# Strassen's scheme for the values' products of layers 2 and 3, with a limit on the ratio of the softmax sums

## The chip, the cores and the metric

One core of a Trainium2 chip runs the whole program. The metric is the device time of one execution, in microseconds (us).

## The reference

Four layers act on x of 2 images, 512 channels and 32 x 32 pixels, in float32. Layer 0 is a deformable attention block with an MLP, layer 1 an attention of eight heads. The change concerns layers 2 and 3, attentions of one head over 1024 pixels:

```python
# layer 2
xn = _group_norm(x, gamma, beta)
q, k, v = split(einsum('oc,bchw->bohw', w_qkv, xn) + b_qkv)
attn = softmax(einsum('bci,bcj->bij', q, k) * C ** (-0.5), axis=-1)
out = einsum('bcj,bij->bci', v, attn)
x = x + einsum('oc,bchw->bohw', w_proj, out) + b_proj
# layer 3
q = einsum('dc,bcn->bdn', wq, f) + bq      # 64 rows; wq, wk, wv ~ 0.05 * normal
k = einsum('dc,bcn->bdn', wk, f) + bk
v = einsum('dc,bcn->bdn', wv, f) + bv
attn = softmax(einsum('bdi,bdj->bij', q, k), axis=1)      # no scale
x = gamma * einsum('bci,bij->bcj', v, attn) + x
```

## The kernel before

The program has three parts. `layer0` (L137) does layer 0's attention; `layers` (L1043) does its MLP and layers 1 to 3; `general` (L851) is a second way of doing layers 1 to 3, and is entered only if a flag says so. In `layer0` and `layers` each engine issues its instructions in the order in which the code writes them (`in_order`, L59). In `general` the framework chooses each engine's order.

`layers` takes the exponentials of the scores without subtracting a maximum. With one image at a time, layer 2 computes scores for eight slices of 128 keys (L1551, a product over 512 channels), ScalarE takes their exponentials into four tiles `ps` of two slices each (L1552), and VectorE adds the tiles up (`sums_of`, L1532, and `summed`, L1345) into `acc`. `values` (L1318) has made `vT`, eight slices of keys by 512 channels. In layer 3 `exponentials` (L1409) makes the scores in pairs of 64-row products that lie in the two halves of the array, and the values' products are issued in between (L1581 to L1587).

`weigh` (L1510) then multiplies: for each half of 512 pixels and each of four blocks of 128 channels, eight products over the keys' slices add up in PSUM (L1517, issued by `accumulate`, L135). `reciprocals_of_both` (L1373), called behind the first block, adds `acc` over the partitions on TensorE with a matrix of ones (`den2`), and VectorE takes the reciprocals. VectorE multiplies each block by the reciprocal and adds bias and x (L1523, L1524); in layer 3 a DMA from SP stores it (`store`, L1590). The iterator that `weigh` is lets layer 2's first image advance the second image's group norm (`norms[2]`) between blocks.

`note` (L1352) writes the least and the greatest reciprocal of each `r` into the next column of `span`: eight columns from layer 1 (two images, four pairs of heads; `divide`), two from layer 2, two from layer 3. Before the last block of layer 3, L1597 to L1602 make `lim` 1 on each partition where all reciprocals lie between e^-64 and e^40. A product with ones (`pn`, L1605) counts the partitions, L1606 turns that into `flag` = 128 - count, every engine loads it at L1618, and

```python
    bad = nc.values_load(flag[0:1, 0:1], min_val=0, max_val=P)
    with tc.If(bad != 0):
        with ExitStack() as g:
            general(g)
```

`general` loads x, as it was after layer 0, from a copy in HBM (`x_d`, L855) and all weights anew on SP's queue. It computes layers 1 to 3 with `attend` (L943): for each tile of 128 queries

```python
                    nc.vector.tensor_reduce(nm, sc, AX.X, ALU.max)                                   # L958
                    nc.vector.tensor_scalar(nm, nm, -scale, None, ALU.mult)
                    nc.scalar.activation(p, sc, AF.Exp, bias=nm, scale=scale, accum_out=sm)          # L962
                    nc.vector.reciprocal(sm, sm)
                    nc.gpsimd.tensor_scalar(p, p, sm, 1.0, ALU.mult, ALU.mult)                       # L964
```

stand between the scores (L956; two PSUM buffers, `ps_s`) and eight transposes on TensorE (L969), which ScalarE and VectorE copy in halves (L972, L974) into `pT`; four such tiles are then weighed with the values (L980). In layer 1 it does so for each of the eight heads and both halves of the pixels.

Of the kernel before, what the change touches and what calls it, by code (L numbers as in the profile page):

```python
# [11 lines left out]
F32 = mybir.dt.float32  # L12
AF = mybir.ActivationFunctionType
ALU = mybir.AluOpType
AX = mybir.AxisListType
# [3 lines left out]
P = 128  # L19
B, C, H, W = 2, 512, 32, 32  # L20
HW = H * W
CC = C // P
HALF = 512
# [56 lines left out]
def kernel(ctx: ExitStack, tc: tile.TileContext, a: dict, out: bass.AP):  # L80
    nc = tc.nc
# [3 lines left out]
    wa = ctx.enter_context(tc.tile_pool(name="wa", bufs=1))  # L85
# [16 lines left out]
    xs = []  # L102
# [5 lines left out]
    s2 = const.tile([P, CC], F32, name="s2")  # L108
    nc.vector.tensor_scalar(s2, col("bn2_g", 0, CC), BN_S, None, ALU.mult)

    def load_w(pool, tag, parts):

        w = pool.tile([P, 4 * HID], F32, name=tag, tag=tag)
        views, at = [], 0
        for src in parts:
            k, n = src.shape[0] // P, src.shape[1]
            v = w[:, at : at + k * n].rearrange("p (k n) -> p k n", n=n)
            for kk in range(k):
                nc.sync.dma_start(out=v[:, kk, :], in_=src[kk * P : (kk + 1) * P, :])
            views.append(v)  # L120
            at += k * n
        return views


    def drain(steps):
        for _ in steps:
            pass

    def advance(steps, n=1):
        for _ in range(n):  # L130
            next(steps, None)

    def accumulate(pm, pairs):
        for k, (w, m) in enumerate(pairs):
            nc.tensor.matmul(pm, w, m, start=(k == 0), stop=(k == len(pairs) - 1))  # L135
# [907 lines left out]
    def layers(f, fold_d, t2_b, o2_b):  # L1043
# [3 lines left out]
        small = f.enter_context(tc.tile_pool(name="small", bufs=2))  # L1047
        keep = f.enter_context(tc.tile_pool(name="keep", bufs=1))
        chan = f.enter_context(tc.tile_pool(name="chan", bufs=4))
        ps_m = f.enter_context(tc.tile_pool(name="ps_m", bufs=2, space=PSUM))  # L1050
# [7 lines left out]
        ones = keep.tile([P, P], F32, name="ones1")  # L1058
        nc.gpsimd.memset(ones, 1.0)
        NSUM = 12  # L1060
        span = keep.tile([P, 2, NSUM], F32, name="span")
# [52 lines left out]
        GN_STATS = CC + 3  # L1114
# [6 lines left out]
        with ExitStack() as mlp:  # L1121
# [8 lines left out]
            ps = mlp.enter_context(tc.tile_pool(name="mlp_ps", bufs=3, space=PSUM))  # L1130
# [39 lines left out]
            def product(pm, i, left, right, cols):  # L1170
                l, r = left[i - 1], right[i - 1]
                accumulate(pm, [(l[:, k, cols], r[:, k, :]) for k in range(l.shape[1])])
# [60 lines left out]
            for c in range(MC):  # L1233
                for m in (MC + c, c):
                    pm = ps.tile([P, BLK], F32, name="pmp", tag="pma")
# [4 lines left out]
            for m in (2, 3, 0, 1):  # L1240
                pm = ps.tile([P, BLK], F32, name="pmp2", tag="pmb")
# [4 lines left out]
            for blk in range(1, NBLK):  # L1246
                b = blk * BLK // HW
# [8 lines left out]
                for c in range(MC + 1):  # L1256
                    if c < MC:
                        pms = products(left1, right1, slice(c * P, (c + 1) * P), (1, 2, 6, 7, 5, 4, 3))
                        p1 = first_of(pms)
# [57 lines left out]

        def values(w, h, vT, bias=None, scale=None):  # L1318

            for s in range(8):  # L1320
                pm = ps_m.tile([P, C], F32, name="pmv", tag="mm")
                accumulate(pm, [(h[k][:, s * P : (s + 1) * P], w[:, k, :]) for k in range(CC)])
                if bias is not None:
                    nc.vector.tensor_add(vT[:, s, :], pm, bias)
                elif scale is not None:
                    nc.scalar.mul(vT[:, s, :], pm, scale)
                else:
                    nc.scalar.copy(vT[:, s, :], pm)
                yield
# [22 lines left out]
        def note(r):  # L1352
            i = next(seen)
            nc.vector.tensor_reduce(span[:, 0, i : i + 1], r, AX.X, ALU.min)
            nc.vector.tensor_reduce(span[:, 1, i : i + 1], r, AX.X, ALU.max)

        def divide(o, acc):
# [11 lines left out]
            nc.vector.tensor_mul(o, o, r)  # L1369
            note(r)  # L1370
            yield

        def reciprocals_of_both(acc):  # L1373

            r = rp.tile([P, HW], F32, name="r")
            den = ps_v.tile([P, HW], F32, name="den2", tag="pv")
            for half in range(2):
                n = slice(half * HALF, (half + 1) * HALF)
                accumulate(den[:, n], [(ones, acc[:, part, n]) for part in range(2)])
                nc.scalar.copy(r[:, n], den[:, n])  # L1380
                nc.vector.reciprocal(r[:, n], r[:, n])
            return r

        wb_stack.close()
        fold2 = f.enter_context(tc.tile_pool(name="fold2", bufs=1))
# [5 lines left out]
        outs = f.enter_context(tc.tile_pool(name="outs", bufs=5))  # L1391
# [113 lines left out]
        vT = new_v()  # L1505
        drain(values(v2, h2s[0], vT))
        drain(add_projection(xs[1], proj1, "proj_b", os_[1]))
        q3, k3, v3 = load_w(wa, "wa", [a["wq3"], a["wk3"], a["wv3"]])

        def weigh(x, vT, ps, acc, bias, done):  # L1510

            r = None
            for half in range(2):
                n = slice(half * HALF, (half + 1) * HALF)
                for m in range(CC):
                    pm = ps_m.tile([P, HALF], F32, name="pw2", tag="mm")
                    accumulate(  # L1517
                        pm, [(vT[:, s, m * P : (m + 1) * P], ps[s // 2][:, s % 2, n]) for s in range(8)]
                    )
                    if r is None:  # L1520
                        r = reciprocals_of_both(acc)
                    y = yp.tile([P, HALF], F32, name="y")
                    nc.vector.tensor_mul(y, pm, r[:, n])  # L1523
                    nc.vector.scalar_tensor_tensor(x[:, m, n], y, bias[:, m : m + 1], x[:, m, n], ALU.add, ALU.add)  # L1524
                    done(m, n)
                    if (half, m) == (0, 3):
                        note(r)
                    yield

        yp = f.enter_context(tc.tile_pool(name="yp", bufs=2))  # L1530

        def sums_of(ps):  # L1532
            acc = accp.tile([P, 2, HW], F32, name="acc")
            for j in range(1, len(ps)):
                summed(acc, ps[j], ps[0] if j == 1 else None)
            return acc

        for b in range(B):
            if b == 1:
                drain(t2(1))  # L1540
                vT = new_v()
                drain(values(v2, h2s[1], vT))
            t, h = t2_of[b], h2s[b]
            ps = []
            for s in range(8):
                if s % 2 == 0:
                    ps.append(pp_.tile([P, 2, HW], F32, name="p"))
                sc = ps_s.tile([P, HW], F32, name="score2", tag="s")
                for half in range(2):
                    n = slice(half * HALF, (half + 1) * HALF)  # L1550
                    accumulate(sc[:, n], [(h[k][:, s * P : (s + 1) * P], t[k][:, n]) for k in range(CC)])  # L1551
                nc.scalar.activation(ps[-1][:, s % 2, :], sc, AF.Exp, scale=C ** -0.5)  # L1552
            for _ in weigh(xs[b], vT, ps, sums_of(ps), o2_b, lambda m, n: None):
                if b == 0:
                    next(norms[2], None)


        def project_both(h, r):
# [13 lines left out]
        for b in range(B):  # L1572
            x = xs[b]
            h = [x[:, cc, :] for cc in range(CC)]
            qk = qkp.tile([P, HW], F32, name="qk", tag="qk")
            project_both(h, qk)
            kq = qkp.tile([P, HW], F32, name="kq", tag="qk")
            for lo in (0, 64):
                nc.sync.dma_start(out=kq[lo : lo + 64], in_=qk[64 - lo : 128 - lo])
            vT = new_v()  # L1580
            steps = values(v3, h, vT, scale=col("gamma3"))  # L1581
            advance(steps, 2)
            ps = []
            for j in range(4):
                left = [slice((2 * j + part) * P, (2 * j + part + 1) * P) for part in range(2)]
                ps.append(exponentials((kq, qk), (qk, kq), left, 1.0))
                advance(steps, 1 + j % 2)  # L1587
            acc = sums_of(ps)

            def store(m, n, x=x, b=b):  # L1590
                nc.sync.dma_start(out=out[b, m * P : (m + 1) * P, n], in_=x[:, m, n])

            steps = weigh(x, vT, ps, acc, gb3, store)
            advance(steps, 6)
            if b == 1:

                lim = small.tile([P, 2], F32, name="lim")  # L1597
                nc.vector.tensor_reduce(lim[:, 0:1], span[:, 0, :], AX.X, ALU.min)
                nc.vector.tensor_reduce(lim[:, 1:2], span[:, 1, :], AX.X, ALU.max)
                nc.vector.tensor_scalar(lim[:, 0:1], lim[:, 0:1], float(np.exp(-64.0)), None, ALU.is_ge)  # L1600
                nc.vector.tensor_scalar(lim[:, 1:2], lim[:, 1:2], float(np.exp(40.0)), None, ALU.is_le)
                nc.vector.tensor_mul(lim[:, 0:1], lim[:, 0:1], lim[:, 1:2])  # L1602
                advance(steps)
                pn = ps_v.tile([1, 1], F32, name="pn", tag="pv")
                nc.tensor.matmul(pn, lim[:, 0:1], ones[:, 0:1], start=True, stop=True)  # L1605
                nc.vector.tensor_scalar(flag, pn, -1.0, float(P), ALU.mult, ALU.add)  # L1606
            drain(steps)
# [99 lines left out]
```

## Time and profile before

| | us |
|---|---|
| runs of the kernel | 3490.8, 3491.4, 3492.2 (median 3491.4) |
| the profiled execution | 3489.9 |
| its span, first to last instruction | 3488.1 |
| TensorE busy | 3452.3 |
| VectorE, ScalarE, GpSimd busy | 2477.1, 1756.1, 492.5 |
| layer 2, from the first image's scores | 2990.2 |
| layer 3, from the first image's projection | 3276.0 |

Times in views count from the span's start. A row names line, engine, operation, what it writes and reads by the program's names, shape and count; then its busy time in us and the mean of one in ns; then the engine's idle time ahead of it, and who ended it. A row of the chain of waits has its start, its length and what ran. TensorE's records overlap, so that the pace of a row of products is read from the chain and not from a record's length. A row of a table of windows has the window and its length, the busy us (and instructions) of PE, PE's weight loads, DVE, ACT and POOL, the granted clock, the DMA engines' busy share and GB/s.

### The profile page before, as it was taken

The numbers are of one execution on the slowest core, as the hardware profiler recorded it, in microseconds if no ns is written. First come the engines' busy times: TensorE is split into PE (matmuls) and PEld (weight loads), VectorE is DVE, ScalarE is ACT, GpSimd is POOL, SyncE is SP. The second block draws the span as 40 slices with busy tenths as digits, with TensorE's granted clock in tenths as the row PEclk, the third lists the DMA queues.
The fourth block names the chain that finished last, engine by engine and source line by source line (L and its number), as shares of the span: only waits on it lengthen the run. The fifth ranks groups of instructions, "written<-read, shape, count | busy, mean of one in ns | idle before, by whom it ended". The sixth has DMA issues, their size and how long they took to land.

```text
span 3488.1 us, 58691 instructions
## 1 busy us (share of the span) xinstructions
PE 3452.3 (99%) x24257; PEld 1446.7 (41%) x24257; DVE 2477.1 (71%) x2731; ACT 1756.1 (50%) x2479; POOL 492.5 (14%) x579
## 2 busy tenths in 40 slices
PE   9999999999999999999999999999999999999999
PEld 4333333333333333333333369999433333444443
DVE  7999999999996999999999835455264374130223
ACT  5767867867764868768676612112243242011110
POOL 1222222222221222222222200000001000000000
PEclk9999999999999999999999999999999999999999
DMA  5676676666664666766776620001100000000000
GB/s 173 148 151 141 139 154 137 150 145 138 149 146 94 144 148 133 151 140 141 152 152 139 143 83 9 14 13 56 33 1 0 1 1 0 15 0 0 6 30 25
DMA packets 134067, 313.65 MB, mean 90 GB/s; under 512 B 21152, under 2 KB 66592, under 8 KB 133024
## 3 DMA queue, kind: packets, MB, share of 16 engines
q0 software_dynamic: 56880, 199.79, 30.1%
q1 hardware_dynamic: 76768, 109.50, 9.8%
q8 instruction: 193, 3.16, 0.4%
q14 instruction: 82, 0.67, 0.1%
q10 hardware_dynamic: 144, 0.52, 0.0%
HBM read 65.17 MB, written 10.75 MB: 22 GB/s over the span
## 4 chain that ended last, share of the span: by engine, by line
PE 77%; DVE 16%; issue 4%; ACT 2%; DMA 0%; DVEq 0%; SPq 0%; POOL 0%; ACTq 0%; POOLq 0%
PE z L534 32%; DVE wa L517 6%; PE pw L135 6%; PE pm L1306 5%; PE pma L135 5%; PE pmv L135 5%; DVE h L548 5%; PE pmb L135 4%; PE score L1417 4%; PE score L135 3%; PE pv L1465 3%; DVE h L517 2%; PE ppr L1337 2%; PE pmp L135 2%; PE pp L620 1%
## 5 line engine op out<-in xcount | busy, mean ns | idle before, releaser
L534 PE MATMUL z<-wa,cpb_w 128*32 128x512 f32 x11904 | 1779.1, 593 | 6.7 <-DVE simbias L481 3.4
L543 ACT ACTIVATE h<-z,b2h 128x1024 f32<-128x1024 f32 x1024 | 1135.3, 1115 | 529.6 <-PE z L534 506.1
L534 PE MATMUL z<-h,cpb_w 128*32 128x512 f32 x4480 | 986.3, 593 | 3.4 <-ACT h L543 2.2
L517 DVE CUSTOM_DVE_ANT_1 wa<-tab,tab 128x1024 f32<-128x1024 f32 x744 | 878.5, 1216 | 34.0 <-PE z L534 33.9
L534 PEld LDWEIGHTS z<-wa,cpb_w 128*32 128x32 f32 x11904 | 493.0, 110 | 883.6 <-issue 803.6
L548 DVE SCALAR_TENSOR_TENSOR h<-h,turn,h 128x1024 f32<-128x1024 f32 x512 | 653.6, 1277 | 8.8 <-ACT h L543 8.6
L534 PEld LDWEIGHTS z<-h,cpb_w 128*32 128x32 f32 x4480 | 256.3, 110 | 334.4 <-issue 291.3
L822 POOL DMA_DIRECT2D h<-h x255 | 226.6, 889 | 1060.6 <-DVE h L548 714.8
L517 DVE CUSTOM_DVE_ANT_1 h<-tab,tab 128x1024 f32<-128x1024 f32 x280 | 333.1, 1217 | 11.4 <-PE z L534 11.2
L1418 ACT ACTIVATE p<-score 128x1024 f32<-128x1024 f32 x144 | 139.5, 1021 | 184.8 <-PE score L1417 184.8
L135 PE MATMUL pw<-p,vT 128*128 128x512 f32 x512 | 221.8, 593 | 1.3 <-DVE y L1523 1.3
L1348 DVE TENSOR_TENSOR acc<-acc,p 128x2048 f32<-128x2048 f32 x56 | 128.8, 2300 | 105.1 <-ACT p L1418 57.8
L1201 ACT COPY p<-pma 128x128 f32<-128x128 f32 x70 | 18.6, 265 | 304.1 <-PE pma L135 304.1
L1350 DVE TENSOR_TENSOR acc<-p 128x2048 f32<-128x2048 f32 x12 | 27.5, 2291 | 183.6 <-ACT p L1552 110.0
L815 POOL DMA_DIRECT2D h<-h x126 | 109.0, 865 | 343.4 <-DMA h<-h 339.8
L135 PEld LDWEIGHTS pw<-p,vT 128*128 128x128 f32 x512 | 97.0, 190 | 122.6 <-issue 121.0
L1193 DVE TENSOR_TENSOR upper<-pma,p 128x256 f32<-128x256 f32 x70 | 29.6, 423 | 163.2 <-ACT p L1201 163.2
L819 POOL DMA_DIRECT2D h<-h x126 | 120.2, 954 | 122.5 <-DMA h<-h 117.5
L1108 POOL TENSOR_SCALAR hc<-x,sc,sh 128x1024 f32<-128x1024 f32 x16 | 28.1, 1765 | 706.1 <-DVE sh L1104 509.4
L1417 PE MATMUL score<-q,k 64*128 64x512 f32 x512 | 127.2, 615 | 0.0
L1306 PE MATMUL pm<-hc,wa 128*64 128x512 f32 x512 | 122.4, 603 | 0.0
L1465 PE MATMUL pv<-p,vT 128*64 128x512 f32 x512 | 121.4, 595 | 0.0
(316 smaller groups left out, 3239.3 us busy)
## 6 DMA issues: line engine op xcount, KB each, us to landing
h<-h POOLq DMA_DIRECT2D x255, 512.0 KB, 4.9
h<-h POOLq DMA_DIRECT2D x252, 256.0 KB, 4.9
tab<-slog_d SPq DMA_DIRECT2D x128, 256.0 KB, 4.5
h<-h SPq DMA_DIRECT2D x126, 256.0 KB, 2.3
wa<-in_qkv_w SPq DMA_DIRECT2D x8, 768.0 KB, 7.5
xt<-in_xt SPq DMA_DIRECT2D x8, 512.0 KB, 7.7
wa<-in_mlp_w SPq DMA_DIRECT2D x4, 1024.0 KB, 7.9
wb<-in_mlp_w SPq DMA_DIRECT2D x16, 256.0 KB, 5.5
```

The costliest lines, as they stand in the source:

```text
L135: nc.tensor.matmul(pm, w, m, start=(k == 0), stop=(k == len(pairs) - 1))
L517: nc.vector._custom_dve(TENSOR_ADD_SAT, out=h1.rearrange("p (y x) -> p y x", x=W), in0=tx[:, quad, point, :].unsqueeze(1).to_broadcast([P, ...
L534: nc.tensor.matmul(z[point * 32 : point * 32 + 32, n], cpb_w2[:, lo : lo + 32], h1s[point][:, n], start=True, stop=True,)
L543: nc.scalar.activation(h2, z, AF.Relu, bias=b2h[:, part : part + 1])
L548: nc.vector.scalar_tensor_tensor(h2, h2, turn[:, part // 2 : part // 2 + 1], parts.pop(part + 1), ALU.mult, ALU.add)
L819: nc.gpsimd.dma_start(out=joins[i - 3][1:P:2], in_=joins.pop(i - 2)[1:P:2], accum_op=ALU.add)
L822: nc.gpsimd.dma_start(out=joins[i - 1], in_=other, accum_op=ALU.add)
L1306: nc.tensor.matmul(pm[at : at + wide], w[:, k, lo + at : lo + at + wide], h[k][:, n], start=(k == 0), stop=(k == CC - 1),)
L1348: nc.vector.tensor_add(acc, acc, p)
L1417: nc.tensor.matmul(sc[:, part, :], ks[part][r, left[part]], qs[part][r, n], start=True, stop=True)
L1418: nc.scalar.activation(p[:, :, n], sc, AF.Exp, scale=scale)
L1465: nc.tensor.matmul(pv[part * 64 : part * 64 + 64, n], vT[:, ls, lo : lo + 64], lp[:, part, n], start=(ls == 0), stop=(ls == 7),)
```

## The change

The key slices and the channels on one side, and the pixels on the other, are each split in two: vT into A11 (slices 0 to 3, channels 0 to 255), A12 (slices 4 to 7, channels 0 to 255), A21 and A22 (channels 256 to 511), the exponentials into B11, B12 (slices 0 to 3, pixels 0 to 511 and 512 to 1023), B21 and B22. Seven products of such halves and sums of them replace the eight. VectorE forms the sums of vT (`form_left`), four slices of `spare`, the unused end of the weights' tile, holding three of them and one lying in A21's place; it forms the sums of the exponentials in place, one of them in `spare`; and it adds the products up. `values` makes its slices in the order 0, 4, 1, 5, 2, 6, 3, 7. The second image's group norm advances during the first image's scores. `reciprocals_of_both` goes; its instructions stand in `weigh`, and the second half's reciprocal comes later. A second condition on the reciprocals joins the flag's.

```diff
-            for s in range(8):
+            for s in (0, 4, 1, 5, 2, 6, 3, 7):
...
+        s1v, s2v, s4v = [spare[:, k * HW : (k + 1) * HW].rearrange("p (k n) -> p k n", k=4) for k in range(3)]
+        t2p = spare[:, 3 * HW : 5 * HW].rearrange("p (k n) -> p k n", k=4)
...
+        def form_left(vT, chunks=range(4)):
+            for k in chunks:
+                a11, a21, a12, a22 = vT[:, k, LO], vT[:, k, HI], vT[:, 4 + k, LO], vT[:, 4 + k, HI]
+                nc.vector.tensor_tensor(s1v[:, k], a21, a22, ALU.add)
+                nc.vector.tensor_tensor(s2v[:, k], s1v[:, k], a11, ALU.subtract)
+                nc.vector.tensor_tensor(a21, a11, a21, ALU.subtract)
+                nc.vector.tensor_tensor(s4v[:, k], a12, s2v[:, k], ALU.subtract)
...
+            rights = {
+                1: right(0, n1), 2: right(1, n1), 3: right(1, n2), 4: right(1, n1),
+                5: right(0, n1), 6: [t2p[:, k] for k in range(4)], 7: right(0, n2),
+            }
+            def product(pm, i, m):
+                accumulate(pm, [(lefts[i][k][:, m * P : (m + 1) * P], rights[i][k]) for k in range(4)])
+            def finished(m, n, in0, in1):
+                y = yp.tile([P, HALF], F32, name="y")
+                nc.vector.tensor_tensor(y, in0, in1, ALU.add)
+                nc.vector.tensor_mul(y, y, r[:, n])
+                nc.vector.scalar_tensor_tensor(x[:, m, n], y, bias[:, m : m + 1], x[:, m, n], ALU.add, ALU.add)
+                done(m, n)
...
+            for m in range(2):
+                pm = ps_m.tile([P, HALF], F32, name="pw1", tag="mm")
+                product(pm, 1, m)
+                nc.scalar.copy(p1[:, m], pm)
+                if m == 0:
                     yield
+            form(b11, b12, b11)
+            form(t2, b22, b11)
...
+            nc.vector.reciprocal(r[:, n1], r[:, n1])
+            yield
+            for m in range(2):
+                pm = ps_m.tile([P, HALF], F32, name="pw2", tag="mm")
+                product(pm, 2, m)
+                finished(m, n1, pm, p1[:, m])
+                yield
+            nc.vector.reciprocal(r[:, n2], r[:, n2])
+            form(b12, b22, b12)
+            form(b21, b21, t2)
+            note(r)
...
+            ps6 = ps_s.tile([P, 2, HALF], F32, name="pw6", tag="s")
+            for m in range(2):
+                product(ps6[:, m], 6, m)
+                nc.vector.tensor_tensor(v[:, m], ps6[:, m], p1[:, m], ALU.add)
+                yield
...
-            for _ in weigh(xs[b], vT, ps, sums_of(ps), o2_b, lambda m, n: None):
-                if b == 0:
-                    next(norms[2], None)
+                if s % 2:
+                    form_left(vT, [s // 2])
+                if b == 0 and s < GN_STATS:
+                    next(norms[2])
+            for i, _ in enumerate(weigh(xs[b], vT, ps, sums_of(ps), o2_b, lambda m, n: None)):
+                if b == 0 and i == 1:
+                    drain(norms[2])
...
             advance(steps, 2)
+            form_left(vT, [0])
             ps = []
             for j in range(4):
...
                 advance(steps, 1 + j % 2)
+                if j:
+                    form_left(vT, [j])
             acc = sums_of(ps)
...
+                near = small.tile([P, 4], F32, name="near")
+                nc.vector.scalar_tensor_tensor(
+                    near, span[:, 0, 8:12], 16.0, span[:, 1, 8:12], ALU.mult, ALU.is_ge
+                )
+                nc.vector.tensor_reduce(lim[:, 1:2], near, AX.X, ALU.min)
+                nc.vector.tensor_mul(lim[:, 0:1], lim[:, 0:1], lim[:, 1:2])
```

Products 3 (in the PSUM buffer of `den2`), 5, 7 and 4 (in the scores' two PSUM buffers, as 6) follow the same way, in the order 1, 2, 3, 6, 5, 7, 4, each with the additions u, v, w that Strassen's scheme (in Winograd's form) asks for.

## The prediction

> **What bounds the kernel now.** I read the page, then the chain of work between 3160 and 3280 us (layer 2, second image), then the users of the tile `flag`.
>
> ```profile
> PE 3452.3 (99%) x24257; PEld 1446.7 (41%) x24257; DVE 2477.1 (71%) x2731; ACT 1756.1 (50%) x2479; POOL 492.5 (14%) x579
> ```
> ```profile
> 3161.72 54.93 PE score L135 x128
> 3216.66 6.87 PE pw L135 x16
> 3223.52 1.73 PE den L135 x4
> 3225.25 0.02 issue
> 3225.28 0.59 ACT r L1380
> 3225.87 0.04 issue
> 3225.91 1.98 PE den L135 x4
> 3227.90 48.07 PE pw L135 x112
> ```
> PE never rests and is the chain. A 128x128x512 float32 product leaves two records: 64 score products are x128 in 54.93 us, so one costs 0.858 us, though a record's row says 593 ns (records overlap). One weighing (`weigh`) is 64 products and the sums' four: 59.3 us. Four exist, 237 us of 3488.
>
> ```profile
> L1606 DVE TENSOR_SCALAR flag<-pn x1: 140/140/140, 3475.4 to 3475.4; 1x1 int32<-1x1 f32 x1
> L1618 PEldq TENSOR_LOAD <-flag x1: 492/492/492, 3475.6 to 3475.6; - x1
> ```
> Every engine loads `flag` at L1618. The trace has no record of L855, L956 or L964: it was 0, and `general` (L851 to L1041), layers 1 to 3 once more with each row's maximum subtracted, was jumped over. **The change makes that jump depend on something new**, so I price both sides.
>
> **What the skill says.** FP8 and Floating Point Precision, TensorE Precision Notes: a true float32 product takes four passes. The trace agrees: 4 x 512 columns at the 2.4 GHz of TensorE: Matmul & The Clock Gate, What's actually happening, are 0.853 us, measured 0.858. SBUF — State Buffer, Who interferes with whom: VectorE holds GpSimd up with two SBUF inputs or a two-port mode, not with reductions or one SBUF input. This trace agrees in size: the same GpSimd instruction (L1108) took 5.11 us for four when little else ran and 8.64 for four beside layer 1. Runtime: NRT & Kernel Launch, Instruction fetch mechanics: a taken branch can stall for its instructions; no run here shows the size.
>
> **Does the guard hold?** `near` is 1 where 16 x the least reciprocal is at least the greatest, for notes 8 to 11. Notes 0 to 7 are layer 1's, 8 and 9 layer 2's, 10 and 11 layer 3's. I worked the sums out from the reference's inputs in float32. Layer 2: 1242 to 2239 and 1252 to 2406, ratios 1.80 and 1.92: hold. Layer 3's scores are not scaled; their deviation is 11.0, and the sums run from 9.3e9 to 1.1e25 (image 0) and 1.0e10 to 8.5e23 (image 1). 16 x 9e-26 is far below 1.1e-10. So `lim` becomes 0, `pn` 0, `flag` 128, and `general` runs after all that the change saves. (The old limits, e^-64 and e^40, hold: 1.1e25 is e^57.7.)
>
> **The change in `layers`.** Seven products of halves, each two column blocks of four: 56 products for 64, so 8 x 0.858 = 6.9 us less per weighing, 27.5 for four. On VectorE 16 `form_left` instructions of 256 columns (0.42 us, as L1149), 6.8 us; four pairs of differences of 1024 (1.22, as L1369), 9.8 us; eight extra 512-column additions (0.69) in `finished`, and six for u, v, w. VectorE is busy 5 to 26% of the 100 us windows from 3100 to 3400 and runs behind PE. Counted from the last score of layer 2: the sums are added up at 3.4; product 1 ends at 6.9 and lets its right side be overwritten, so the differences are ready at 12 and the first half's reciprocal (3.3, L1381) at 15.3; product 2, on PE to 17.2, is used up at 19.6; then the second reciprocal, the other differences and the two span reductions, to 30.3, while PE does products 3 (to 24) and 6 (to 31). v is ready at 31.8, u at 38.7, the last w at 45.5, the last x at 54; PE's last product ends at 51.5. Product 7 asks product 6's PSUM buffer back at 37.8 and product 4 that of 5 at 44.6, after v and u have read them, by 6 us each: nothing waits, and VectorE's work costs nothing, except twice: in layer 3 the three acc additions (2.3 each) now stand behind `form_left([3])`, which waits for the last values' copy (0.7 + 1.7). They end 9.3 us after PE's last values, product 1 covers 6.9, PE waits 2.5. Two such cost 5. The new order of the values and the group norm of the second image (statistics, two small matmuls, four L1108, no transfers; pulled from the weighing into the scores) move under PE's work and pass no DMA; the guard's instructions are three of 0.16; `pn` waits some 0.7, the last x comes 0.7 later. Sum: 27.5 - 5 - 1.4 = **21 us saved**. If a weighing's cover were gone, 6 us late would become a wait: were VectorE 10 us slower in each, the saving would be eaten.
>
> **What `general` costs.** The change does not touch it; its instructions, and each engine's order of them, are those compiled into the kernel before. Products: 288 projections, 192 values, 416 scores, 512 weighings, 128 output projections, 1536 x 0.858 = 1318 us. The heads' 64-row products are issued alone, so at full price (L1417's pairs share the array: 8 records in 1.92 us). 1280 transposes:
>
> ```profile
> 2010.40 0.60 PE L653 MATMUL pt<-cst,simb 128*128 128x128 f32 x4
> ```
> one record each, 0.27 us long but 0.11 apart: 141 us. PE's floor is 1459.
>
> Layer 1 has 32 blocks (8 heads, 2 column halves, 2 images) of four row tiles: scores S 1.72, transposes T 0.88 each, then weighing V 6.86: 17.3 us if PE never waited. Between S and T lie
>
> ```profile
> L588 DVE TENSOR_REDUCE mx<-pt 128x16 f32<-128x1024 f32 x7 | 8.6, 1225 | 6.4 <-PE pt L585 6.4
> L1418 ACT ACTIVATE p<-score 128x1024 f32<-128x1024 f32 x144 | 139.5, 1021 | 184.8 <-PE score L1417 184.8
> ```
> ```profile
> L1108 POOL TENSOR_SCALAR hc<-x,sc,sh x16: 1193/1199/3339, 2416.4 to 3107.3; 128x1024 f32<-128x1024 f32 x16
> ```
> the maximum (1.22), its scaling (0.15, L1600), exp (1.02, and 0.21 to read its sum, L594), a reciprocal (0.2, L664) and the division on GpSimd (1.28: the L1108 set of 5.11, since the maxima and copies read PSUM). PE issues V T0 S3 T1 S4 T2 S5 T3 S6 V (half of S3 and of S4 stand behind T1 and T2), since S has two PSUM buffers; ScalarE issues each copy of T ahead of the exp two tiles on, and VectorE V's store and two copies ahead of reciprocal 2. From V's end: T0 to 0.95, its copy 1.74 and only then exp 2 to 2.97, reciprocal 3.4, division 4.65; T2 4.7 to 5.6; maximum 3 at 5.0, exp 3 at 6.45, which frees S5's buffer: 6.5 to 8.2; T3 to 9.15; exp 4 at 9.35 frees S6: 11.1; V to 18.0. With 0.2 for the hops between engines (0.02 to 0.06 each in the chain above) 18.2 a block; 17.3 is the least, and the longest division gives 21.2 (below).
>
> Layer 1, an image: projections 96 x 0.858 = 82.4, first chain 7 (exp's table 1.28 in it), 16 x 18.2 = 291, last store 1, output projection 27.5: 409. Layer 2: 82.4, PE-bound attention 54.9 + 7 + 54.9, waits 6, 28.5, and its group norm with PE idle 10 (eleven small steps of 0.16 to 0.3, Sqrt's table 1.28, four L1108): 244. Layer 3: 41.2, first chain 7, two blocks of 11.1 + 27.5: 126. Twice each: 818, 488, 252. Layer 1's second norm: 10. The start: `general` waits for x (4.2 MB) and the first weights (3.1 MB).
>
> ```profile
> 2040.00:2053.00 13.00, 12.43 (x56) 10.43 (x57) 6.17 (x18) 4.05 (x7) 2.14 (x4) 1.00 0.97 318
> ```
> They queue on SP behind layer 3's stores. 7.3 MB at 318 GB/s are 23 us; with 2 to land and issue, 26; the later weights hide behind layer 1. The branch's fetch, and the slower clock that the same TensorE page gives after idle spells (seven here), are in no row: 0 to 30, I take 9; a gain is excluded, since nothing is removed. Sum 818 + 488 + 252 + 10 + 26 + 9 = **1603**.
>
> The profiled execution took 3489.9 (span 3488.1); 3489.9 - 21 + 1603 = 5071.9. The median of the runs stands 1.5 above it: **5073**.
>
> **Rivals.** *Guard holds* (my reading of notes or sums is wrong, or the engines' exp differs): 3491.4 - 21 = 3470, faster. It decides at a ratio of 16 in layer 3; the trace doesn't hold the sums, but e^35 against e^2.8 leaves little. Chance 4%; another 1% that it holds and VectorE's cover fails, within 0.2%. *GpSimd held up*: a division at L1108's longest, 3.34, puts T2 at 6.8, T3 at 11.7 and V's end at 21.2; 3 us in 32 + 4 blocks is 108: 5181. For it: the contended sets; against: PSUM inputs. 10%. *PE packs better*: floor 1459 + 26 + norms 30 + chains 36, less 21: 5021. 10%. The likeliest, 75%: GpSimd at up to 2.2 (+25), the unknown 0 to 30, packing halfway: 5035 to 5125. The range, 5015 to 5180, leaves out the first rival and the edges of the next two. 0.2% (7 us) is about what this kernel's measurement tells from no change. Faster 0.04, same 0.01, slower 0.95.
>
> **What would show it.** Rows of L956 x some 830, L969 x1280 and L964 x160 after 3460; a load of x_d; TensorE at some 85 to 90% there; weighings of 112 + 4 records in about 52 us; layer 3's den late by 2.5. No such rows would prove me wrong outright; blocks away from 18.2 us only in size.

## The result, and the profile after

| | us |
|---|---|
| kernel before, median of the runs beside it | 3491.1 |
| changed kernel, median (4 runs, 5171.9 to 5175.9) | 5174.3 |
| ratio, 95% interval | 1.482 (1.4795 to 1.4846) |
| predicted (range) | 5073 (5015 to 5180) |
| the profiled execution, its span | 5174.4, 5172.6 |

The kernel is slower by 1683 us. The forecast of "slower" and its reason, the fallback, hold, and the time lies in the range; but it is 101 us above the number. The page of the changed kernel, its busy row and some of the groups that the kernel before did not have:

```profile
PE 5030.8 (97%) x28561; PEld 2135.4 (41%) x28561; DVE 3043.8 (59%) x3778; ACT 2098.0 (41%) x3051; POOL 693.7 (13%) x755
...
L980 PE MATMUL pav<-pT,vT 128*64 128x512 f32 (+1 forms) x1024 | 462.2, 609 | 0.3 <-DVE pT L974 0.2
L956 PE MATMUL score<-qk 64*128 64x512 f32 (+1 forms) x832 | 424.4, 655 | 7.6 <-ACT p L962 7.2
...
L964 POOL TENSOR_SCALAR p<-p,den 128x1024 f32<-128x1024 f32 x160 | 178.7, 1117 | 1272.2 <-DVE den L963 1078.4
...
L969 PE MATMUL tp<-cst,p 128*128 128x128 f32 x1280 | 192.3, 298 | 33.1 <-POOL p L964 33.1
```

L956 x832, L969 x1280, L964 x160: `general` ran in full. GpSimd's division took 1.117 us in the mean. And the users of the tile `flag`, the answer to the two lines shown of before; the last line is the same load in the kernel before:

```profile
L1705 DVE TENSOR_SCALAR flag<-pn x1: 140/140/140, 3488.7 to 3488.7; 1x1 int32<-1x1 f32 x1
...
L1717 DVEq TENSOR_LOAD <-flag x1: 541/541/541, 3500.4 to 3500.4; - x1
```
```profile
L1618 DVEq TENSOR_LOAD <-flag x1: 535/535/535, 3482.0 to 3482.0; - x1
```

VectorE loads the flag when it has finished layer 3: at 3500.4. In the kernel before it does so at 3482.0. So `layers` ends **18.4 us later**, where the prediction has it 21 earlier: a second error of 39 us, independent of the guard. With the span that ends at 3488.1 before, `general` took 5172.6 - 3488.1 - 18.4 = 1666 us, 63 more than the 1603 predicted. 39 + 63 are the 102 that the profiled execution lies above the 5071.9 of the sum.

Where the 39 come from is seen in layer 2's second image, the stretch whose chain the prediction shows. TensorE's timeline of the changed kernel (start, length, what ran, in brackets the idle time ahead of it and who ended it):

```profile
3221.83 7.03 PE L135 MATMUL pw<-p,vT 128*128 128x512 f32 x16
...
3233.07 7.03 PE L135 MATMUL pw<-p,vT 128*128 128x512 f32 x16
3239.94 7.03 PE L135 MATMUL pw<-p,wa 128*128 128x512 f32 x16
3246.80 3.60 PE L135 MATMUL pw<-wa 128*128 128x512 f32 x8
3253.06 5.40 PE L135 MATMUL pw<-wa 128*128 128x512 f32 x8 [2.66 <-DVE v L1595]
3258.29 3.60 PE L135 MATMUL pw<-p,wa 128*128 128x512 f32 x8
3262.67 3.70 PE L135 MATMUL pw<-p,wa 128*128 128x512 f32 x8 [0.78 <-DVE u L1600]
3266.21 3.60 PE L135 MATMUL pw<-p,vT 128*128 128x512 f32 x8
3271.19 7.13 PE L135 MATMUL pw<-p,vT 128*128 128x512 f32 x16 [1.38 <-DVE y L1557]
3279.10 3.70 PE L135 MATMUL pw<-p,vT 128*128 128x512 f32 x8 [0.78 <-DVE y L1557]
```

Products 1, 2 and 3 run without a break, two halves in one row of x16. From product 6 on each product falls into two rows of x8, and the second half waits for VectorE: for v[0], u[0], y. v[0] is computed at 3252.3, 31 us after the last score, just when the prediction has it; what the prediction did not see is that the second half of product 6 stands still until v[0] has read the first. Behind the wait of 2.66 us the next eight records take 5.40 instead of 3.60, at a granted clock of 0.50. The weighing lasts 60.9 us; 59.3 before, 52.4 predicted.

### The profile page after: what moved, and what is told of

The parts are those of the page before. It is cut to its first block, busy times and chain, and to the rows that moved or that the text cites. A ratio compares the mean times of both kernels' runs of the same rounds, so it can differ in the third digit from the quotient of the medians.

```text
span 5172.6 us, 69557 instructions
## 1 busy us (share of the span) xinstructions
PE 5030.8 (97%) x28561; PEld 2135.4 (41%) x28561; DVE 3043.8 (59%) x3778; ACT 2098.0 (41%) x3051; POOL 693.7 (13%) x755
## 5 line engine op out<-in xcount | busy, mean ns | idle before, releaser
L980 PE MATMUL pav<-pT,vT 128*64 128x512 f32 (+1 forms) x1024 | 462.2, 609 | 0.3 <-DVE pT L974 0.2
L956 PE MATMUL score<-qk 64*128 64x512 f32 (+1 forms) x832 | 424.4, 655 | 7.6 <-ACT p L962 7.2
L822 POOL DMA_DIRECT2D h<-h x255 | 226.1, 887 | 1064.2 <-DVE h L548 717.0
L964 POOL TENSOR_SCALAR p<-p,den 128x1024 f32<-128x1024 f32 x160 | 178.7, 1117 | 1272.2 <-DVE den L963 1078.4
L958 DVE TENSOR_REDUCE nm<-score 128x1 f32<-128x1024 f32 x160 | 195.7, 1223 | 175.2 <-PE score L956 175.1
L980 PEld LDWEIGHTS pav<-pT,vT 128*64 128x64 f32 (+1 forms) x1024 | 169.1, 168 | 289.2 <-issue 286.2
L962 ACT ACTIVATE p<-score,nm 128x1024 f32<-128x1024 f32 x160 | 178.4, 1115 | 264.4 <-DVE nm L959 264.3
L940 DVE TENSOR_TENSOR vT<-pmv,gvbias 128x512 f32<-128x512 f32 x48 | 33.2, 691 | 398.6 <-PE pmv L937 398.6
L969 PE MATMUL tp<-cst,p 128*128 128x128 f32 x1280 | 192.3, 298 | 33.1 <-POOL p L964 33.1
L969 PEld LDWEIGHTS tp<-cst,p 128*128 128x128 f32 x1280 | 151.4, 151 | 165.0 <-POOL p L964 93.9
L956 PEld LDWEIGHTS score<-qk 64*128 64x128 f32 (+1 forms) x832 | 145.3, 198 | 175.0 <-issue 137.7
```

Source lines behind the costliest of these rows:

```text
L822: nc.gpsimd.dma_start(out=joins[i - 1], in_=other, accum_op=ALU.add)
L956: nc.tensor.matmul(sc[:, n], q[:, rows], k[:, n], start=(i == 0), stop=(i == len(qk) - 1))
L969: nc.tensor.transpose(tp[:, i, :], p[:, s * P : (s + 1) * P], ident)
L980: nc.tensor.matmul(pm[:n], vT[:, s, lo : lo + n], pT[s // 4][:, s % 4, :], start=(s == 0), stop=(s == 7))
```

## Experiments

**Which notes set the flag, and what the scheme costs without the fallback.** `guard_l2` asks the ratio of layer 2's notes alone:

```diff
-                near = small.tile([P, 4], F32, name="near")
+                near = small.tile([P, 2], F32, name="near")
...
-                    near, span[:, 0, 8:12], 16.0, span[:, 1, 8:12], ALU.mult, ALU.is_ge
+                    near, span[:, 0, 8:10], 16.0, span[:, 1, 8:10], ALU.mult, ALU.is_ge
```

> The changed kernel with the new limit read over layer 2's two notes alone (span columns 8 and 9), so layer 3's result is formed from sums that lie fifteen orders of magnitude apart and is not replaced. Theory: layer 3's sums set the flag, nothing else; then general is not entered, no row of its lines appears, and the time is that of the changed kernel's own layers 0 to 3, which its trace puts 18.4 us later than before (last x of layer 3 at 3500.4 against 3482.0): 3510 us, slower than before by 0.5%. Rival, the prediction's price for the scheme: 3470. Rival, the flag comes from elsewhere (layer 2's notes, their order): about 5174.

Measured: 3510.0 (5 runs, 3505.4 to 3513.6), ratio to before 1.0058 (1.0044 to 1.0071). Its trace has no row of L956. So layer 3's ratios, and not layer 2's, call `general`; and the scheme alone is slower than the products it replaces. TensorE's waits in it from 2985 us on (us in total, times, longest):

```profile
PE pw L135 <- DVE v L1595: 10.5, 4, 2.7
PE pw L135 <- DVE y L1557: 8.3, 8, 1.4
PE den L135 <- DVE acc L1348: 8.1, 3, 3.4
PE pw L135 <- DVE u L1600: 3.1, 4, 0.8
PE den L135 <- ACT r L1576: 2.7, 4, 0.7
...
```

The last row shown is as before (2.7 in 4 there too). The other four are 30.0 us of new waits, against 27.5 us of products saved. This trace's span is 15.5 us longer than before's; most of the other 13 is the clock, which falls behind some of the waits: eight rows of its timeline, x8 in 5.40 for 3.60 among them, are together 11.6 us longer than at the full clock.

**The fallback alone.** `guard_alone` is the kernel before, with the changed guard (three instructions on VectorE) and nothing else.

```diff
                 nc.vector.tensor_mul(lim[:, 0:1], lim[:, 0:1], lim[:, 1:2])
+                near = small.tile([P, 4], F32, name="near")
+                nc.vector.scalar_tensor_tensor(
+                    near, span[:, 0, 8:12], 16.0, span[:, 1, 8:12], ALU.mult, ALU.is_ge
+                )
+                nc.vector.tensor_reduce(lim[:, 1:2], near, AX.X, ALU.min)
+                nc.vector.tensor_mul(lim[:, 0:1], lim[:, 0:1], lim[:, 1:2])
```

> The kernel before, plus the four guard instructions over notes 8 to 11 and nothing of Strassen's scheme. Theory: the guard alone brings the slowdown; layer 3's sums are the same, general runs after an unchanged layer 3: 5174.3 less the 18.4 us by which the changed layers ended later, 5156. Rival, the scheme's rounding is what makes the ratio fail: 3492.

Measured: 5158.0 (4 runs), ratio 1.4779 (1.4756 to 1.4802). The two parts add up: 3491 + 19 for the scheme + 1667 for the guard are 5177; the changed kernel takes 5174.

**The halves in tiles of their own.** If the second half waits because both halves are one PSUM tile, then two tiles take the waits away, with every instruction and TensorE's order kept. `split_tiles` is `guard_l2`, so it too leaves out the limit on layer 3's sums, with

```diff
-            ps6 = ps_s.tile([P, 2, HALF], F32, name="pw6", tag="s")
             for m in range(2):
-                product(ps6[:, m], 6, m)
-                nc.vector.tensor_tensor(v[:, m], ps6[:, m], p1[:, m], ALU.add)
+                ps6 = ps_s.tile([P, HALF], F32, name="pw6", tag="s")
+                product(ps6, 6, m)
+                nc.vector.tensor_tensor(v[:, m], ps6, p1[:, m], ALU.add)
```

and so for 5, 7 and 4 (5 and 4 in `ps_m`).

> As guard_l2, with each half of products 6, 5, 7 and 4 in a PSUM tile of its own (6 and 7 in the scores' buffers, 5 and 4 in the small ones) in place of two halves of one tile; work and order are the same. Theory: the second half of a product waits for VectorE's reading of the first because both lie in one tile; in the trace of the changed kernel this costs per weighing 2.8 + 1.8 (slower clock after it) at product 6, 1.0 at 5, 1.6 at 7 and 1.1 at 4, 8.3 us, 33 in four: 3510 - 33 = 3477, faster than before by 0.4%. Rival, VectorE's throughput sets the pace (2.9 us of additions against 3.4 of products for a half, and reciprocals, differences and notes ahead of them), so that it only waits elsewhere: 3500 to 3510.

Measured: 3477.9 (5 runs, 3472.5 to 3478.1), ratio 0.996 (0.9947 to 0.9974): 32 us less than `guard_l2`. All of TensorE's waits from 2985 us on that remain:

```profile
PE den L135 <- DVE acc L1348: 8.1, 3, 3.4
PE den L135 <- ACT r L1576: 2.7, 4, 0.7
PE pn L1704 <- DVE lim L1701: 0.6, 1, 0.6
```

The rows of v, u and y are gone, and products 6, 5, 7 and 4 are whole again; layer 2's second image in TensorE's timeline:

```profile
3240.78 7.03 PE L135 MATMUL pw<-wa 128*128 128x512 f32 x16
3247.65 7.03 PE L135 MATMUL pw<-p,wa 128*128 128x512 f32 x16
3254.51 13.90 PE L135 MATMUL pw<-p,vT 128*128 128x512 f32 x32
```

This weighing lasts 52.5 us (3215.80 to 3268.34), the length that the prediction gave it. 5 and 4 changed their pool as well; 6 and 7 kept theirs, and their waits went too.

**VectorE's lateness instead.** The rival: v comes late because VectorE takes `note`'s two reductions (1.21 each) first; a shared tile would not matter if v came in time. `note_late` is `guard_l2` with

```diff
             form(b21, b21, t2)
-            note(r)
...
                 finished(m, n2, ps3[:, m], u[:, m])
+                if m == 1:
+                    note(r)
                 yield
```

> As guard_l2, with note (two reductions of 1.2 us on VectorE) moved from ahead of product 6 to behind the two halves of product 5; tiles as in the change. If VectorE's lateness at product 6 is a cause of its own, the wait for v falls from 2.8 to about 0.5 us and the clock doesn't drop: 4 us a weighing, 16 in all, of which the notes give back 0 to 2 us each at product 7: 3494 to 3502. If only the tiles' halves matter, the other three waits remain and the same follows; if VectorE's throughput is the limit, 3508 to 3510.

Measured: 3504.4 (5 runs), ratio 1.0039 (1.0026 to 1.0053): less than `guard_l2`, but above the window that the theory gave. Its waits:

```profile
PE pw L135 <- DVE y L1557: 13.3, 8, 3.0
...
PE pw L135 <- DVE v L1594: 3.1, 4, 0.8
PE pw L135 <- DVE u L1599: 3.1, 4, 0.8
PE pn L1705 <- DVE lim L1702: 2.9, 1, 2.9
...
```

v's wait shrinks from 2.66 to 0.78 a weighing, and not to nothing: 0.78 is VectorE's addition with the hops around it, and is what a half in a shared tile costs even when VectorE is on time. The rest is given back: product 7's second half now waits 3.0 us (5.0 more in four weighings), and `pn` waits 2.9 for the late notes (0.6 in `guard_l2`). All of TensorE's waits add up to 33.2 us in this trace and to 33.3 in `guard_l2`'s. So VectorE's lateness decides where TensorE waits, and not how long in all; the shared tile is what makes it wait. That the median is 5.6 us lower is not explained by waits; `guard_l2`'s own runs spread over 8 us, and its trace is of the fastest of them.

**Where the fallback's 63 us went.** TensorE's timeline of `guard_alone`, the first head of layer 1:

```profile
3587.43 3.70 PE L956 MATMUL score<-qk 64*128 64x512 f32 x8
3593.49 3.78 PE L956 MATMUL score<-qk 64*128 64x512 f32 x4 [2.37 <-ACT p L962]
3597.20 1.97 PE L969 MATMUL tp<-cst,p 128*128 128x128 f32 x8
```

Four scores' records take 3.78 us, eight of them 3.70 just before: behind the gap of 2.37 us the granted clock is 0.50, and it stays there to the products with the values (`pav`, from 3619.6) and 4 us into them. Four such spells at half clock stand in the trace, at the head of each image in layers 1 and 3; in layer 3 the gap ahead of them is 1.11 us, and not 2.4. `gap_filled` adds, to the first head of each of these,

```diff
+                    if (tb, t4) == full_at:        # (0, 1)
+                        full = ps_m.tile([P, HALF], F32, name="full", tag="mm")
+                        for _ in range(3):
+                            nc.tensor.matmul(full, vT[:, 0, :P], vT[:, 1, :], start=True, stop=True)
```

> The kernel guard_alone (5158: the products as before, the fallback running) with three full products of 128x128x512 that nobody reads, put into TensorE's queue behind the first two row tiles' scores of the first head of each image in layer 1 and of each image in layer 3: four places, where TensorE stood still for about 2.4 us. Theory: the gap is what drops the granted clock to 0.50. Filled (3 x 0.858 = 2.6 us), no drop follows; each spell lasted about 26 us at half clock and lost 13, so the time falls by about 4 x 13 = 52 to some 5106, and scores x4 take 1.98 there and not 3.78. Rival: full products are what holds the clock up, and scores of 64 rows with transposes alone let it fall wherever they run without them for some microseconds; then the spells start a few microseconds later and the time is 5150 to 5162.

Measured: 5119.5 (4 runs, 5119.4 to 5121.2), ratio 1.4669 (1.4647 to 1.4692): 38.6 less than `guard_alone`, of 52 expected. The same place, and layer 3's first image:

```profile
3588.52 3.70 PE L958 MATMUL score<-qk 64*128 64x512 f32 x8
3592.14 2.84 PE L962 MATMUL full<-vT 128*128 128x512 f32 x6
3594.92 1.98 PE L958 MATMUL score<-qk 64*128 64x512 f32 x4
3596.83 1.09 PE L975 MATMUL tp<-cst,p 128*128 128x128 f32 x8
...
4893.22 2.84 PE L958 MATMUL score<-qk 64*128 64x512 f32 x6
4897.16 3.65 PE L958 MATMUL score<-qk 64*128 64x512 f32 x4 [1.10 <-ACT p L968]
```

In layer 1 both spells are gone (mean clock of 3590 to 4030 us: 0.99, 0.95 in `guard_alone`); the stretch from the first score to the end of the first `pav` row is 13.6 us shorter, or 14.0 without the 0.34 by which the filling is longer than the gap. In layer 3 the framework put another order on TensorE: a gap of 1.10 us comes some 8 us later than the one of 1.11 in `guard_alone`, and the clock fell there, for four clock steps of 3.413 us and not eight. The same stretch is only 5.6 us shorter there. Twice 13.6 and twice 5.6 are 38.4; that is why the gain is short of 52.

`full_later` has the three products behind the first row tile's transposes, with those as weights, so that they can't move up:

```diff
                             nc.vector.tensor_copy(dst, tp)
+                    if (tb, t4) == full_at:        # (0, 0)
+                        full = ps_m.tile([P, HALF], F32, name="full", tag="mm")
+                        for _ in range(3):
+                            nc.tensor.matmul(full, pT[0][:, 0, t4 * P : (t4 + 1) * P], vT[:, 1, :], start=True, stop=True)
```

> guard_alone with the same three unread full products in the same four heads, but behind the first row tile's transposes, some 6 to 10 us after the gap, when the clock has dropped. Theory (full products bring the clock back): it is 1.0 again within about 5 us of them, scores x4 take 1.98 from there on; each spell is cut from 26 to about 15 us, 5 us saved, less some 4 us for the products themselves: 5150 to 5160. Rival (once dropped, the clock stays at 0.50 for a fixed time of some 26 us, or until the products of Values): scores x4 stay at 3.78 until Values' products start, and the time is 5158 + 4 x 5 = 5178.

Measured: 5333.4 (2 runs), ratio 1.528 (1.5252 to 1.5308): 175 more than `guard_alone`, outside every expectation, and still the clock answers the question:

```profile
3605.32 4.71 PE L980 MATMUL full<-vT,pT 128*128 128x512 f32 x6
3609.86 1.04 PE L971 MATMUL tp<-cst,p 128*128 128x128 f32 x8
...
3612.91 1.98 PE L958 MATMUL score<-qk 64*128 64x512 f32 x4
...
3630.95 1.98 PE L958 MATMUL score<-qk 64*128 64x512 f32 x4 [1.11 <-ACT p L964]
3632.86 1.87 PE L971 MATMUL tp<-cst,p 128*128 128x128 f32 x8
```

Within the 4.71 us of the full products the clock is back (transposes 1.04, scores 1.98); no fixed time is served. What cost 175 us begins in the last two lines: the framework ordered the heads that follow differently too, their blocks got a gap of 1.11 us ahead of scores (33.5 us in 28 waits from 3590 to 4470, 5.1 in 3 in `guard_alone`), and behind these the clock fell again; its mean there is 0.80 for 0.95. That the added dependence brought the new order about is argued from the edit alone.

`rows_128` asks whether it is the gap alone, or the 64 rows of the scores on both its sides:

```diff
-                attend([(q[m][r], k[m][r])], 64 ** -0.5, vT, [(head * 64, 64)], store)
+                attend([(q[m], k[m])], 64 ** -0.5, vT, [(head * 64, 64)], store)
```

> guard_alone (5158) with the scores of layer 1 in the fallback taken over all 128 rows of the q and k tiles instead of one head's 64: each head then weighs with the scores of its pair of heads added up, which is not what the layer computes. The number of products and their length stay the same, and so does the first gap of 2.4 us in each image. Theory A: what lets the clock stay at 0.50 for some 26 us behind the gap is that products of 64 rows count for less than products of 128; with 128 rows the clock comes back within some microseconds, as in layer 2's attention, and the two spells in layer 1 shrink from 13 us lost to about 3 each: 5136 to 5142. Theory B: the transposes and short runs of scores don't bring it back however many rows they have; both spells stay and the time is 5156 to 5160.

Measured: 5110.4 (4 runs, 5109.7 to 5111.6), ratio 1.4645 (1.4621 to 1.467): 47.6 less than `guard_alone`. Theory A's direction, and more than A's size:

```profile
3594.76 1.98 PE L956 MATMUL score<-qk 128*128 128x512 f32 x4 [2.37 <-ACT p L962]
...
3608.14 7.08 PE L980 MATMUL pav<-pT,vT 128*64 128x512 f32 x16
...
3626.41 7.08 PE L980 MATMUL pav<-pT,vT 128*64 128x512 f32 x16
```

The same gap of 2.37 us, and the clock does not fall at all in layer 1's two heads. Two spells of 14 us are 28. The rest is a second thing: a block of four row tiles now takes 3626.41 - 3608.14 = 18.3 us, and 18.9 with 64 rows (3608.97 to 3627.87 in `gap_filled`, at full clock); 32 blocks by 0.63 are 20. 28 + 20 are 48, and 47.6 were measured. TensorE's waits for the division in this stretch fall from 16.9 to 9.4 us.

**A version that beats both.** `best_l2` uses the scheme in layer 2 alone, where the sums lie within a factor of two, and asks the guard for these two ratios; layer 3 keeps its old `weigh`. Besides `split_tiles`' tiles, the exponentials' additions are issued in the score loop, and den stands behind product 2's first half:

```diff
+                if s == 2:
+                    acc = accp.tile([P, 2, HW], F32, name="acc")
+                elif s > 2 and s % 2:
+                    summed(acc, ps[-1], ps[0] if s == 3 else None)
...
+            product(pm2[0], 2, 0)
             r = rp.tile([P, HW], F32, name="r")
             den = ps_v.tile([P, HW], F32, name="den2", tag="pv")
             for n in (n1, n2):
                 accumulate(den[:, n], [(ones, acc[:, part, n]) for part in range(2)])
-                nc.scalar.copy(r[:, n], den[:, n])
+            nc.scalar.copy(r, den)
+            product(pm2[1], 2, 1)
```

> Strassen's level in layer 2 alone, where the sums lie within a factor of two; layer 3's products as before; guard on layer 2's two ratios alone. Each half of products 6, 5, 7 and 4 has its own PSUM tile. The exponentials' additions are issued between the scores, both halves of den run before ScalarE's copy and behind product 2's first half. Theory: the two weighings take about 52 us each; before had 61.5 (with the second norm's two products in it) and 59.4, so some 16 us less, of which the norm's products, moved into the scores, give 0.6 back: 3491 - 15.5 = 3475. Rival: VectorE, with the left sums, the additions and the norm in the score loop, is late to the first den or to product 6 in the first image, as in split_tiles (den waited 3.4 us there): 3478 to 3481. Every output is computed in full.

Measured: 3471.9 (5 runs, 3471.0 to 3472.0), before 3490.3; ratio 0.9946 (0.9933 to 0.996): **18.5 us faster than the kernel before**, 3 better than the theory. Layer 2's first image in TensorE's timeline, which has no wait in it:

```profile
3045.55 10.46 PE L135 MATMUL pw<-p,vT 128*128 128x512 f32 x24
3055.86 3.60 PE L135 MATMUL den<-acc,ones 128*128 128x512 f32 x8
3059.29 3.60 PE L135 MATMUL pw<-p,vT 128*128 128x512 f32 x8
3062.72 7.03 PE L135 MATMUL pw<-p,wa 128*128 128x512 f32 x16
...
3083.32 13.90 PE L135 MATMUL pw<-p,vT 128*128 128x512 f32 x32
```

51.5 us to 3097.05, where the next product starts: 60 products by 0.858, nothing else. Before, this weighing took 61.5 (norm and waits in it), the second 59.4. The two are 17.8 us shorter. Of these, 13.7 are the 16 products fewer; the other 4 are waits and the norm's two products, of which this order might have relieved the old products as well. No run has the order without the scheme.

## Why the prediction was right and wrong

- **TensorE is the chain, a product costs 0.858 us:** right; `best_l2`'s weighings are 60 x 0.858. (The 0.853 set beside it is an estimate from the two pages of the Trainium skill named there.)
- **The guard fails by layer 3's sums:** right; `guard_l2` and `guard_alone` each show a side of it. The sums themselves stand in no trace. Without this step the forecast would have had the wrong sign.
- **The scheme saves 21 us in `layers`: the step that failed.** It was argued that "Product 7 asks product 6's PSUM buffer back at 37.8 ...: nothing waits". The question was put for the next owner of the buffer only. Within one product the second half waits until VectorE has read the first half, since both are one tile. Up to there VectorE's times were right (v at 31 us), the products saved were as counted, and the two den waits in layer 3 were 2.4 each (2.5 predicted). Not in it were the 21.9 us of waits for v, u and y, a third den wait of 3.4 in layer 2's first image, and the slower clock behind these, 11.6: 36.9 of the 39 us. The third den wait is a second, smaller step that failed: the norm moved into the scores was put at nothing, but its steps stand ahead of the sums in VectorE's queue and wait there for TensorE's small products (30 us for the first), so that the first sum starts at 3044.4 in `guard_l2`, after the last score. In `best_l2`, which issues the sums between the scores, this wait is gone. Beside GpSimd's part of the norm each sum then takes 3.1 us for 2.3, and GpSimd's four instructions 9.5 for 5.3 in the kernel before. The line to read was among those shown: in the chain of before, the second half of den waits for ScalarE's copy of the first (0.59 and the hops), and den2 is one tile for both. The Trainium skill, Perfetto Trace Analysis, Matmuls, advises rotating groups of products through different PSUM banks so that the reading of one lies beside the next. These halves already lay in different banks by their size (512 float32 values each; PSUM — Partial Sum Buffer, Specifications (TRN2), gives a bank as many), and the second still waited; `split_tiles` shows that, in this program, what counts is the tile.
- **`general` costs 1603 us:** mechanism right, 63 us short. By its terms, in the trace of the changed kernel: layer 1 with the norm that follows 443.5 an image (409 + 10 predicted), layer 2 242 with a norm and 237 without (244 and 234), layer 3 140 and 144 (126 each), start 22 (26); of the start, 6 lie beside the last store, with which the span of before ends. Of the 49 us in layer 1, 28 are two clock spells and some 20 the 0.63 that a block takes more with 64-row scores; in layer 3 two more spells are 27 (half of eight steps each). The term mis-sized is the 9 us for fetch and slow clock: the four spells alone are 55. The 18.2 of a block came out at 18.3, once the scores had 128 rows as those from which the prediction took its times; the rows of that block show no idle time of TensorE, so it is not shown that the 0.9 above 17.3 are the waits which the prediction has for it.
- **The range:** 5174 lies in it by luck. The likeliest band, 5035 to 5125, misses it, and the upper end, 5180, was set by the GpSimd rival, which did not come about; both errors, 39 and 63, went the same way.
- **Rivals.** *Guard holds, 3470*: `guard_l2` is that case for the scheme, and it is 3510, not faster; the rival shared the failed step. *GpSimd held up, 5181*: the time is near, the reason is not, since the division took 1.117 us, and 3.34 was needed. *PE packs better, 5021*: the time is 153 us above it.

## What to carry to other kernels

Before a tile is given to two results that are read one after the other, ask who reads the first and when: in this program the writer of the second waited for it, and one tile for each result cost nothing, as the buffers were there. Work out a guard's condition from the data before pricing what it guards. And where the products that follow a gap use half the rows, price the gap with the slower clock behind it: 2.37 us of standing still cost 14 more here.

## What the runs showed of the hardware

A gap of 2.37 us, or of 1.1, among 64-row scores took the granted clock to 0.50, and it stayed there through 22 to 26 us of unbroken such scores and transposes; full products brought it back (three of them within 4.7 us). With 128-row scores on both sides the same 2.37 us cost nothing. In the changed kernel's weighing, among full products, a gap of 2.66 us cost 1.8 us (x8 in 5.40 for 3.60), and the next row was at full pace again. The Trainium skill, TensorE: Matmul & The Clock Gate, What's actually happening, has the clock fall after an idle window of about 3.4 us and return after a busy one of as much. The length agrees: in the ten traces of this case each spell at 0.50 lasts a whole number of steps of 3.413 us, one to nine, unless the program ends first. What decides differs on both ends: the clock fell behind steps in which TensorE worked for up to 0.69 of the time, and seven or eight steps of unbroken 64-row scores and transposes did not bring it back. Two pairs of such steps, the first two rows from `guard_alone`, the others from `rows_128`:

```profile
3589.35:3592.77 3.42, 1.77 (x5) 0.46 (x3) 2.76 (x4) 1.82 (x2) 0.00 (x0) 1.00 0.00 0
3592.77:3596.18 3.41, 2.69 (x3) 1.16 (x4) 0.33 (x2) 1.76 (x4) 2.21 (x2) 0.50 0.00 0
```
```profile
4010.06:4013.48 3.42, 1.74 (x5) 0.44 (x3) 2.75 (x4) 1.83 (x2) 0.00 (x0) 1.00 0.01 2
4013.48:4016.89 3.41, 2.70 (x13) 1.69 (x14) 1.00 (x3) 1.75 (x4) 2.21 (x2) 1.00 0.00 0
```

TensorE is busy for the same time in both first steps (1.77 and 1.74 us), with 64 rows in one and 128 in the other, and the clock falls behind the first alone. So the rows count, and not time alone. All steps of the ten traces can be counted in this way: each record of 512 columns as 0.429 us, each transpose as 0.11, twice that at half clock, and a product of 64 rows as half. Then the 123 steps at full clock behind which it fell are filled to at most 0.35, and the 12148 others to at least 0.36. Counted by time alone the two overlap (falls up to 0.69, others from 0.39), and so they do with transposes left out (0.34 and 0.11). At half clock, the 121 steps before a return are filled to 0.74 or more, the 222 others to 0.77 or less. This is read from these traces alone. It fits the long spells: unbroken 64-row scores with transposes fill a step to between the two marks (0.49 to 0.71 in `guard_alone`'s first spell), and so keep the clock that they find. It also says when a gap costs nothing: 2.66 us within one step of `guard_l2` left 0.28 of it, and the clock fell; 2.59 us that a step's border cut in two left 0.55 and 0.61, and it did not. By the same count (an estimate) 2.37 us wholly within one step would leave 0.30 even with 128 rows, so where the borders lay helped `rows_128`.

The 0.63 us that a block takes more with 64-row scores has no single row to show for it. TensorE's waits for the division differ by 7.5 us in this stretch (16.9 and 9.4), of the 20. And where transposes of 128 rows are followed by scores of 64, the starts lie 1.02 us apart instead of 0.88 to 0.93; that the change of rows is the reason is not shown. How the 0.63 divides stays open.
